# More tiles and filling products around the recurrence of a convolution-attention hybrid

## The chip, the cores and the metric

The kernel runs on one core of one Trainium2 chip. The time is that of one execution on the device in microseconds (us). It was measured three times before the change: 1805.73, 1807.35 and 1809.59 us, median 1807.35. The profile is of one further execution, with a span of 1804.1 us from the first to the last instruction.

## The reference, cut to what matters

```python
# x: 8 x 128 x 48 x 48, N = 48 * 48 = 2304 tokens of 128 channels for each of 8 batches
x = x + causal_attention(group_norm(x))        # layer 0, with projections q, k, v
t = to_tokens(x)                               # 8 x 2304 x 128
t = t + softmax(h @ h.T) @ h                   # layer 1, h = layernorm(t)
# layer 1, the recurrence over the 2304 tokens
Wx  = layernorm(t) @ W.T
Wx  = (Wx - mean) * rsqrt(var + 1e-5) * gamma + beta    # mean, var over all batches and tokens
y_k = sigmoid(Wx_k + y_(k-1) @ V.T),   y_0 = 0
out = t + y
```

Everything is computed in 32-bit floating point.

## The kernel before, in words

**Attention.** Batches follow one another. In each, a causal and then a full attention run over six chunks of 384 queries (`NQ` = 6, `QC` = 384). One list of products (`stream`) is issued with a lag of three items between a score product and its use. The rest of the work (norms, projections, transposes, residuals) hangs in chains of steps, and a planner (`Stream`, `st`) keeps an estimated clock and issues a chain's next step between two products when its due time has come. The numbers in `st.add` and `st.then` are the planner's estimates in us. Nothing reorders the instructions after that: `manual_schedule` keeps the order in which the code issues them, on each engine.

**The last chunks.** `Full.after` builds a chain for each chunk of the full attention: `sums`, `residual` (writes t2, the tokens after layer 1's attention), `rooted` (GpSimd's inverse root for the layer norm), and then, for the last two chunks of the last batch, `keep_last` (transposes t2 to channels by tokens and stores it to `t2_d` in DRAM), `normed`, `back` and `statistics` (the product with W, `wx`, its statistics on VectorE and its copy on ScalarE). The other chunks go by way of DRAM, `spread`, `fetch`, `product`, `stored`. In `product`, chunks 0 and 1 of each batch (the tokens of the recurrence's group 0) are also copied by step into `t2c` by `keep`, and `store` sends them to the output.

**The recurrence.** The 2304 tokens are cut into 96 segments of `LS` = 24 steps, which run side by side in three groups of 32 (`SG`), 8 batches each, so that one step of one group is a product of 128 x 256 columns. Each segment first runs `WARM` = 12 steps over the end of the segment before it, and at the end `seams` compares the states at the cuts; if they disagree, or if a bound on the logits (`bound`, `fl`) is exceeded, a flag makes the kernel take its general path. A step of a group is: TensorE's product into a bank z that VectorE has filled with the normed inputs (`inputs`, two steps at a time), then ScalarE's sigmoid into a tile y.

The results leave in two ways. For group 0 the tokens are already in the output for steps up to `LM` = 20, and GpSimd issues a transfer that adds y, four steps at a time (line 1484). For groups 1 and 2 `add_residual` (line 1458) adds the tokens t2s, loaded back from `t2_d`, on GpSimd into a tile r, two steps at a time, and SyncE sends r (line 1459). Of the last four steps all three groups are added by `add_residual`, on VectorE. SyncE issues its transfers in the order of the code.

The tiles that hold these things are pools with a fixed number of buffers: three tiles y of four steps in group 0, five of two steps in groups 1 and 2, three tiles r for GpSimd and three for VectorE. A writer of a tile waits until the last reader of the buffer is done, a transfer included.

```python
for g in (1, 2, 0):                                       # line 1388
    for b in range(0, B, 4):
        nc.sync.dma_start(t2s[g][:, b : b + 4], t2_d[:, b : b + 4, ts(g, SG * LS)])
```

TensorE's clock is granted by a throttle, at full or half rate. Before the first work of the kernel there are twelve products of the identity with itself (`idle`, line 1329).

Of the kernel before, what the change touches and what calls it, by code (L numbers as in the profile page):

```python
# [14 lines left out]
F32 = mybir.dt.float32  # L15
AF = mybir.ActivationFunctionType
ALU = mybir.AluOpType
AX = mybir.AxisListType
# [10 lines left out]
LOGIT_BOUND = 60.0  # L29
# [575 lines left out]
def fast_path(ctx: ExitStack, tc: tile.TileContext, x, pe, w_ffn, out, x_tok, w_qkv, w_pos, v_t, gamma_beta, flag):  # L605
    nc = tc.nc
    B, C, H, W = x.shape
    N = H * W
    P = 128
# [4 lines left out]
    NQ = N // QC  # L614
    QB = QC // P
    SCALE = 1.0 / math.sqrt(P)
# [5 lines left out]
    dpool = ctx.enter_context(tc.tile_pool(name="dram", bufs=1, space=DRAM))  # L622


    LS = N // SEGS
    SG = SEGS // SEG_GROUPS
    SJ = QC // LS
# [2 lines left out]
    t2_d = dpool.tile([P, B, N], F32, tag="t2_d", name="t2_d")  # L630
    LM = LS - 4

    posb_d = dpool.tile([P, NQ, 3, QC], F32, tag="posb_d", name="posb_d")


# [3 lines left out]
    ident = cpool.tile([P, P], F32, tag="ident", name="ident")  # L639
    make_identity(nc, ident)  # L640
    ones = cpool.tile([P, 1], F32, tag="ones", name="ones")
# [5 lines left out]
    bound = cpool.tile([P, B], F32, tag="bound", name="bound")  # L647
# [12 lines left out]
    with ExitStack() as actx:  # L660
# [9 lines left out]
        work1 = actx.enter_context(tc.tile_pool(name="work1", bufs=1))  # L670
# [6 lines left out]
        def psum_s(name):  # L677
            return ps_s.tile([P, CH], F32, tag="s", name=name)

        def psum_t(name):  # L680
            return ps_t.tile([P, CH], F32, tag="t", name=name)
# [19 lines left out]
        def load_x(b, pieces=2):  # L701
# [12 lines left out]
            out=grp3, in_=grp3, compare_op=ALU.is_ge, fill=0.0, base=0, pattern=[[-cg, GROUPS], [0, cg]], channel_multiplier=1  # L714
        )
        nc.gpsimd.affine_select(
            out=grp3, in_=grp3, compare_op=ALU.is_ge, fill=0.0, base=cg - 1, pattern=[[cg, GROUPS], [0, cg]], channel_multiplier=-1
# [5 lines left out]
            out=triu, in_=triu, compare_op=ALU.is_ge, fill=0.0, base=0, pattern=[[1, P]], channel_multiplier=-1  # L723
# [28 lines left out]
        for r in range(1 - R, R):  # L752
            nc.gpsimd.affine_select(
                out=same, in_=same, compare_op=ALU.not_equal, fill=1.0, base=r * SQ, pattern=[[0, R], [-1, SQ]], channel_multiplier=1
# [4 lines left out]
            out=mine, in_=mine, compare_op=ALU.is_ge, fill=0.0, base=0, pattern=[[0, NQ - 1], [-SQ, R], [0, QB]], channel_multiplier=1  # L759
        )  # L760
        nc.gpsimd.affine_select(
            out=mine, in_=mine, compare_op=ALU.is_ge, fill=0.0, base=SQ - 1, pattern=[[0, NQ - 1], [SQ, R], [0, QB]], channel_multiplier=-1
# [8 lines left out]
        st = Stream()  # L771
# [298 lines left out]
        class Full:  # L1070
# [115 lines left out]
            def after(self, j, o):  # L1186
                b, rows, tsum = self.b, self.rows, self.tsum
# [45 lines left out]
                def rooted():  # L1233
                    c["rs"] = roots[j % 2]
                    nc.gpsimd.tensor_tensor(c["rs"][:, :QB], c["ve"], mhalf, ALU.pow)  # L1235

                def turn_root():
                    nc.vector.transpose(roots_t[j % 2], c["rs"])
# [16 lines left out]
                def product():  # L1255
                    if j < SG // SJ:
                        keep(c["t2x"])
                        st.then(st.now, [("ACT", 0.75)])
                    tp = psum_t(f"wx_{b}_{j}")
                    nc.tensor.matmul(tp[:, :QC], w1T, c["t2x"], start=True, stop=True)  # L1260
                    nc.vector.tensor_mul(c["scale"], tp[:, :QC], c["scale"])
                    nc.vector.bn_stats(stats[:, b * NQ + j, :], c["scale"])

                def stored():
                    store()
                    nc.scalar.copy(wx[:, :, b, ts(j, SJ)], c["scale"].rearrange("p (s l) -> p l s", l=LS))
# [7 lines left out]
                def keep(t2x):  # L1274

                    if before is not None:
                        st.finish(before)
                    if j == 0:
                        self.t2c = work1.tile([P, LM, SG], F32, tag="t2c", name=f"t2c_{b}")
                    nc.scalar.copy(self.t2c[:, :, ts(j, SJ)], t2x.rearrange("p (s l) -> p l s", l=LS)[:, :LM])  # L1280

                def store():
                    if j == SG // SJ - 1:
                        nc.sync.dma_start(out[0, :, :LM, b, :], self.t2c)

                def back():
                    tp = turned_back(c["x2"], f"tx_{b}_{j}")
# [3 lines left out]
                def statistics():  # L1291
                    tp = psum_t(f"wx_{b}_{j}")
                    nc.tensor.matmul(tp[:, :QC], w1T, c["xc"], start=True, stop=True)
                    nc.vector.bn_stats(stats[:, b * NQ + j, :], tp[:, :QC])
                    nc.scalar.copy(wx[:, :, b, ts(j, SJ)], tp[:, :QC].rearrange("p (s l) -> p l s", l=LS))

# [5 lines left out]
                if last:  # L1302
                    steps = [
                        (keep_last, 0.35, [("ACT", 0.5)]),
                        (normed, 0.0, [("DVE", 1.1)]),
                        (back, 0.35, [("ACT", 0.5)]),
                        (statistics, QC * US, [("DVE", 0.55), ("ACT", 0.85)]),
                    ]
                else:
                    steps = [  # L1310
                        (turn_root, 0.0, [("DVE", 0.15)]),
                        (spread, 0.0, [("", 10.0)]),
                        (fetch, 0.0, [("", 9.0)]),
                        (product, QC * US, [("DVE", 1.0)]),
                        (stored, 0.0, [("ACT", 0.85)]),
                    ]
                c["chain"] = self.before["chain"] = st.add([
                    (sums, 0.15, [("DVE", 0.8)]),
                    (residual, 0.35, [("DVE", 3.2)]),
                    (rooted, 0.0, [("POOL", 0.9)]),  # L1320
                    *steps,
                ], max(at, st.free["DVE"]) + 0.2 - st.now)

        norm_chain = {}
        st.add([(ffn_weights, 0.3, [("DVE", 0.5)])], 30.0)

        for i in range(12):
            tp = psum_t(f"idle_{i}")
            nc.tensor.matmul(tp[:, :P], ident, ident, start=True, stop=True)
        for j in range(3):  # L1330
            positions(0, j)
        gn = st.add(group_norm(0))
# [22 lines left out]
        for n in range(len(stream) + LAG):  # L1355
            if n < len(stream):
                part, j, what, first, last = stream[n]
                ready[n] = part.begin(j, what, first)
            if n >= LAG:
                part, j, what, first, last = stream[n - LAG]  # L1360
# [12 lines left out]
    G = SEG_GROUPS  # L1373
    TZ = 2
    TO = [4] + [2] * (G - 1)
    assert LS * SEGS == N and WARM % TZ == 0 and LS % TO[0] == 0 and SG * B * TZ == CH
    with ExitStack() as rctx:
        rc = rctx.enter_context(tc.tile_pool(name="rconst", bufs=1))
        rst = [rctx.enter_context(tc.tile_pool(name=f"rst{g}", bufs=3 if g == 0 else 5)) for g in range(G)]
        rres = rctx.enter_context(tc.tile_pool(name="rres", bufs=3))  # L1380
        ps_z = [rctx.enter_context(tc.tile_pool(name=f"ps_z{g}", bufs=2, space=PSUM)) for g in range(G)]
        ps_w = rctx.enter_context(tc.tile_pool(name="ps_w", bufs=1, space=PSUM))

        rctx.enter_context(tc.manual_schedule())


        t2s = [rc.tile([P, B, SG * LS], F32, tag=f"t2s_{g}", name=f"t2s_{g}") for g in range(G)]
        for g in (1, 2, 0):
            for b in range(0, B, 4):
                nc.sync.dma_start(t2s[g][:, b : b + 4], t2_d[:, b : b + 4, ts(g, SG * LS)])  # L1390
        t2_g = [t.rearrange("p b (s l) -> p l b s", l=LS) for t in t2s]

        zero = rc.tile([P, CH], mybir.dt.bfloat16, tag="zero", name="zero")
        nc.gpsimd.memset(zero, 0.0)

        pw = ps_w.tile([P, CH], F32, tag="w", name="pw")
        nc.tensor.matmul(pw[0:1, :B], ones[:, 0:1], bound, start=True, stop=True)
        fl = rc.tile([1, 4], F32, tag="fl", name="fl")
        nc.vector.reduce_max(fl[:, 0:1], pw[0:1, :B], AX.X)
        nc.vector.tensor_scalar(fl[:, 1:2], fl[:, 0:1], LOGIT_BOUND / SCALE, None, ALU.is_gt)  # L1400


        zs = [deque() for _ in range(G)]
        banks = [deque() for _ in range(G)]
        for t in range(-WARM, -WARM + 2 * TZ, TZ):
            for g in range(G):
                z = ps_z[g].tile([P, TZ, B, SG], F32, tag="z", name=f"z_{g}_{t}")
                nc.tensor.matmul(z.rearrange("p t b s -> p (t b s)"), zero[:, :P], zero, start=True, stop=True)
                banks[g].append(z)

        mv = rc.tile([P, 2], F32, tag="bn_mv", name="bn_mv")
        nc.vector.bn_aggr(mv, stats)
# [40 lines left out]
            nc.vector.tensor_reduce(dm[:, g : g + 1], d[:, g, :, :n], AX.XY, ALU.max, apply_absolute_value=True)  # L1453

        def add_residual(g, l0, yt):
            engine = nc.gpsimd if l0 < LM else nc.vector
            r = rres.tile([P, TZ, B, SG], F32, tag=f"r_{l0 < LM}", name=f"r_{g}_{l0}")
            engine.tensor_add(r, yt, t2_g[g][:, l0 : l0 + TZ])  # L1458
            nc.sync.dma_start(out[g, :, l0 : l0 + TZ], r)

        for t in range(-WARM, LS):
            s = t % TZ
            for g in range(G):
# [12 lines left out]
                if s == TZ - 1:  # L1476
                    zs[g].popleft()

                    l0 = t + 1 - TZ
# [11 lines left out]
        for g in range(G):  # L1491
            add_residual(g, LS - TZ, y[g][:, TO[g] - TZ :])
            if g:
                continue
            nc.tensor.matmul(pw[0:1, P : P + 1], off, ones[:, 0:1], start=True, stop=True)
            nc.vector.tensor_scalar(flag, pw[0:1, P : P + 1], fl[:, 1:2], 0.5, ALU.add, ALU.is_gt)
# [56 lines left out]
```

## Time and profile before

| stretch, us | what runs | TensorE busy | VectorE | ScalarE | GpSimd | granted clock |
|---|---|---|---|---|---|---|
| 0 to 1709.3 | both attentions of 8 batches | 1697.34 | 1233.02 | 702.82 | 178.50 | 1.00 |
| 1709.3 to 1723.3 | last chunk's chain, statistics | 6.94 | 7.05 | 3.19 | 2.69 | 0.61 |
| 1723.3 to 1778.6 | 36 steps of three groups | 51.88 | 45.89 | 41.11 | 28.16 | 0.91 |
| 1778.6 to 1796.1 | last sums, seams, flag | 0.19 | 15.10 | 0.00 | 9.06 | 0.56 |
| 1796.1 to 1804.1 | last transfer, reading the flag, end | 0.00 | 0.01 | 0.00 | 0.00 | 0.50 |

Each row is a stretch of the one profiled execution, with the busy time of the engines in it in us. The granted clock is a mean; 1.00 is the full rate and 0.50 the half one. Busy time beside other busy time costs nothing: what counts in each row is which engine, transfer or wait is the last to let the next row begin. A long busy time is no sign of it by itself.

### The profile page before, as it was taken

The numbers are of one execution on the slowest core, as the hardware profiler recorded it, in microseconds if no ns is written. First come the engines' busy times: TensorE is split into PE (matmuls) and PEld (weight loads), VectorE is DVE, ScalarE is ACT, GpSimd is POOL, SyncE is SP. The second block draws the span as 40 slices with busy tenths as digits, with TensorE's granted clock in tenths as the row PEclk, the third lists the DMA queues.
The fourth block names the chain that finished last, engine by engine and source line by source line (L and its number), as shares of the span: only waits on it lengthen the run. The fifth ranks groups of instructions, "written<-read, shape, count | busy, mean of one in ns | idle before, by whom it ended". The sixth has DMA issues, their size and how long they took to land.

```text
span 1804.1 us, 21863 instructions
## 1 busy us (share of the span) xinstructions
PE 1756.3 (97%) x6291; PEld 1102.3 (61%) x6291; DVE 1301.1 (72%) x3321; ACT 747.1 (41%) x1852; POOL 218.4 (12%) x305
## 2 busy tenths in 40 slices
PE   9999999999999999999999999999999999999893
PEld 5666566666666566665665566665666656665572
DVE  5868678766877678686787668786686767866376
ACT  2344334443344423443245433444335433454362
POOL 1100012000210012000110001100120001200035
PEclk8999999999999999999999999999999999999987
DMA  4205752258304682067513493046720674035776
GB/s 149 103 4 185 202 155 67 92 162 214 112 33 145 177 206 84 17 190 200 139 66 105 153 234 115 6 152 183 193 84 37 190 193 115 27 118 171 174 259 163
DMA packets 173461, 242.43 MB, mean 134 GB/s; under 512 B 62001, under 2 KB 142034, under 8 KB 173332
## 3 DMA queue, kind: packets, MB, share of 16 engines
q1 hardware_dynamic: 172380, 237.93, 44.6%
q0 software_dynamic: 720, 2.62, 1.0%
q8 instruction: 52, 0.85, 0.2%
q14 instruction: 77, 0.63, 0.1%
q10 hardware_dynamic: 232, 0.40, 0.1%
HBM read 144.99 MB, written 95.88 MB: 134 GB/s over the span
## 4 chain that ended last, share of the span: by engine, by line
PE 95%; DVE 2%; DMA 1%; issue 1%; ACT 0%; POOL 0%; SPq 0%; DVEq 0%; ACTq 0%; POOLq 0%
PE s L1166 18%; PE o L1180 18%; PE s L978 17%; PE o L989 16%; PE o L1176 13%; PE pj L869 4%; PE pj L872 2%; PE wx L1260 2%; PE tb L929 1%; PE oc_t L929 1%; PE of_t L929 1%; PE z L1470 1%; DVE r L1458 0%; PE pb L827 0%; DMA out_dram<-r 0%
## 5 line engine op out<-in xcount | busy, mean ns | idle before, releaser
L1168 ACT ACTIVATE p<-s,shift 128x384 f32<-128x384 f32 x504 | 292.2, 580 | 492.6 <-PE s L1166 483.7
L1166 PE MATMUL s<-xh 128*128 128x384 f32 x1008 | 410.3, 489 | 0.0
L980 ACT ACTIVATE p<-s 128x384 f32<-128x384 f32 (+2 forms) x504 | 232.4, 461 | 425.8 <-PE s L978 391.7
L1180 PE MATMUL o<-p,xhT 128*128 128x384 f32 x1008 | 403.9, 487 | 4.4 <-ACT p L1168 4.4
L978 PE MATMUL s<-q,k 128*128 128x384 f32 (+2 forms) x1008 | 381.1, 460 | 0.1
L989 PE MATMUL o<-p,vT 128*128 128x384 f32 (+2 forms) x1008 | 377.6, 456 | 0.0
L1176 PE MATMUL o<-g,xhT 128*128 128x384 f32 x720 | 281.2, 488 | 0.8 <-DMA g<-e 0.8
L1180 PEld LDWEIGHTS o<-p,xhT 128*128 128x128 f32 x1008 | 189.0, 190 | 132.2 <-ACT p L1168 8.7
L989 PEld LDWEIGHTS o<-p,vT 128*128 128x128 f32 x1008 | 188.8, 190 | 114.7 <-issue 0.6
L1166 PEld LDWEIGHTS s<-xh 128*128 128x128 f32 x1008 | 186.1, 190 | 115.0
L1004 DVE TENSOR_TENSOR acc<-acc,p 128x384 f32<-128x384 f32 (+2 forms) x408 | 211.0, 517 | 48.8 <-ACT p L980 17.9
L978 PEld LDWEIGHTS s<-q,k 128*128 128x128 f32 x1008 | 180.6, 191 | 90.5 <-issue 0.5
L1129 DVE STREAM_TRANSPOSE t<-p 128x384 f32<-128x384 f32 x360 | 187.2, 550 | 37.5 <-ACT p L1168 34.6
L1176 PEld LDWEIGHTS o<-g,xhT 128*128 128x128 f32 x720 | 133.2, 190 | 82.9 <-issue 1.7
L1137 DVE TENSOR_REDUCE tsum<-t 128x12 f32<-128x1152 f32 x120 | 162.4, 1353 | 4.2
L874 DVE TENSOR_TENSOR z<-pj,pb 128x384 f32<-128x384 f32 x144 | 79.0, 549 | 103.5 <-PE pj L869 87.7
L983 POOL TENSOR_TENSOR p<-p,triu 128x128 f32<-128x128 f32 x144 | 83.5, 587 | 545.8 <-ACT p L980 434.4
L1235 POOL TENSOR_TENSOR roots<-ve_f,mhalf 128x3 f32<-128x3 f32 x48 | 40.7, 849 | 552.5 <-DVE ve_f L913 552.5
L1168 ACT ACTIVATION_READ_ACCUMULATOR p<-s,shift 128x1 f32 x504 | 97.2, 193 | 0.0
L869 PE MATMUL pj<-xn,wT 128*128 128x384 f32 x192 | 79.8, 500 | 1.4 <-DVE xn L862 1.4
L919 POOL TENSOR_TENSOR rs_c<-ve_c,mhalf 128x3 f32<-128x3 f32 x48 | 46.9, 976 | 245.7 <-DVE ve_c L913 245.7
L1222 DVE SCALAR_TENSOR_TENSOR t<-of_t,ri,t1t 128x128 f32<-128x128 f32 x144 | 41.5, 344 | 33.2 <-PE of_t L929 33.2
(257 smaller groups left out, 1485.7 us busy)
## 6 DMA issues: line engine op xcount, KB each, us to landing
e<-t SPq DMA_DIRECT2D x120, 576.0 KB
g<-e SPq DMA_DIRECT2D x480, 144.0 KB
pb<-posb_d SPq DMA_DIRECT2D x46, 576.0 KB
t1t<-in_x_tok_dram SPq DMA_DIRECT2D x48, 192.0 KB
t2s<-t_d SPq DMA_DIRECT2D x6, 1536.0 KB
t_d<-tt SPq DMA_DIRECT2D x184, 48.0 KB
t2x<-t_d SPq DMA_DIRECT2D x46, 192.0 KB
scale<-rs SPq DMA_DIRECT2D x46, 192.0 KB
```

What stands on the lines that cost most here:

```text
L869: nc.tensor.matmul(ps[:, :QC], wT[:, j, :], xn, start=True, stop=True)
L978: nc.tensor.matmul(s[:, off:QC], keys[b][:, ts(m, P)], queries[b, j][:, off:], start=True, stop=True)
L980: nc.scalar.activation(p[:, off:], s[:, off:QC], AF.Exp, scale=SCALE)
L983: nc.gpsimd.tensor_mul(p[:, off : off + P], p[:, off : off + P], triu)
L989: nc.tensor.matmul(o[:, off:QC], vals[b][:, ts(m, P)], p[:, off:], start=first, stop=last)
L1004: nc.vector.tensor_add(a[:, off:], a[:, off:], p[:, off:])
L1129: nc.vector.transpose(t[:, :, :, g, :].rearrange("p b j r -> p j b r"), p.rearrange("p (j b r) -> p j b r", j=QB, b=R))
L1137: nc.vector.tensor_reduce(self.tsum[j][:, n - j - 1, :], t.rearrange("p b j m r -> p (b j) (m r)"), AX.X, ALU.add)
L1166: nc.tensor.matmul(s[:, :QC], xh[:, ts(m, P)], xh[:, ts(j, QC)], start=True, stop=True)
L1168: nc.scalar.activation(p, s[:, :QC], AF.Exp, bias=shift, accum_out=self.rows[:, m, j : j + 1])
L1176: nc.tensor.matmul(out_ap, xhT[:, QB * i + g, :], p, start=first, stop=last)
L1180: nc.tensor.matmul(o[:, :QC], xhT[:, what[1], :], p, start=first, stop=last)
```

## The change

It is meant to take waits out of the recurrence and of the stretch before it, and to keep TensorE's clock at its full rate there. It has these parts:

- In the two gaps of the last chunk's chain, and between the clearing of the banks z and the first step, products of the identity are issued on TensorE: 14, 8 and 14 of them. The twelve at the start stay, in one tile of another pool.
- The product for the logits' bound and the two VectorE instructions that read it move from before the statistics' sum to behind the first inputs.
- `t2c` keeps all 24 steps; the copy has 384 elements a partition instead of 320, and the planner's cost for it goes from 0.75 to 0.85. The last four steps are stored by step in `t2l_d`. The recurrence loads them as `t2l`, so t2s is not loaded for group 0, and group 0's adds on VectorE read contiguous tokens.
- Group 0 has four tiles y instead of three, groups 1 and 2 have six instead of five, GpSimd's results have six tiles r instead of three; VectorE's three are in a pool of their own.

```diff
+    t2l_d = dpool.tile([P, LS - LM, B, SG], F32, tag="t2l_d", name="t2l_d")
...
                 def rooted():
                     c["rs"] = roots[j % 2]
                     nc.gpsimd.tensor_tensor(c["rs"][:, :QB], c["ve"], mhalf, ALU.pow)
+                    if b == B - 1 and j == NQ - 1:
+                        idle(psum_s("idle_last"), 14)
...
-                        st.then(st.now, [("ACT", 0.75)])
+                        st.then(st.now, [("ACT", 0.85)])
...
-                        self.t2c = work1.tile([P, LM, SG], F32, tag="t2c", name=f"t2c_{b}")
-                    nc.scalar.copy(self.t2c[:, :, ts(j, SJ)], t2x.rearrange("p (s l) -> p l s", l=LS)[:, :LM])
+                        self.t2c = work1.tile([P, LS, SG], F32, tag="t2c", name=f"t2c_{b}")
+                    nc.scalar.copy(self.t2c[:, :, ts(j, SJ)], t2x.rearrange("p (s l) -> p l s", l=LS))
...
-                        nc.sync.dma_start(out[0, :, :LM, b, :], self.t2c)
+                        nc.sync.dma_start(out[0, :, :LM, b, :], self.t2c[:, :LM])
+                        nc.sync.dma_start(t2l_d[:, :, b, :], self.t2c[:, LM:])
...
                     nc.tensor.matmul(tp[:, :QC], w1T, c["xc"], start=True, stop=True)
+                    if b == B - 1 and j == NQ - 1:
+                        idle(psum_s("idle_last2"), 8)
                     nc.vector.bn_stats(stats[:, b * NQ + j, :], tp[:, :QC])
...
-        for i in range(12):
-            tp = psum_t(f"idle_{i}")
-            nc.tensor.matmul(tp[:, :P], ident, ident, start=True, stop=True)
+        def idle(tp, n):
+
+            for _ in range(n):
+                nc.tensor.matmul(tp[:, :P], ident, ident, start=True, stop=True)
+
+        idle(psum_s("idle"), 12)
...
-        rst = [rctx.enter_context(tc.tile_pool(name=f"rst{g}", bufs=3 if g == 0 else 5)) for g in range(G)]
-        rres = rctx.enter_context(tc.tile_pool(name="rres", bufs=3))
+        rst = [rctx.enter_context(tc.tile_pool(name=f"rst{g}", bufs=4 if g == 0 else 6)) for g in range(G)]
+        rres = rctx.enter_context(tc.tile_pool(name="rres", bufs=6))
+        rlast = rctx.enter_context(tc.tile_pool(name="rlast", bufs=3))
...
-        for g in (1, 2, 0):
+        for g in range(1, G):
             for b in range(0, B, 4):
                 nc.sync.dma_start(t2s[g][:, b : b + 4], t2_d[:, b : b + 4, ts(g, SG * LS)])
+        t2l = rc.tile([P, LS - LM, B, SG], F32, tag="t2l", name="t2l")
+        nc.sync.dma_start(t2l, t2l_d)
...
-        nc.tensor.matmul(pw[0:1, :B], ones[:, 0:1], bound, start=True, stop=True)
-        fl = rc.tile([1, 4], F32, tag="fl", name="fl")
-        nc.vector.reduce_max(fl[:, 0:1], pw[0:1, :B], AX.X)
-        nc.vector.tensor_scalar(fl[:, 1:2], fl[:, 0:1], LOGIT_BOUND / SCALE, None, ALU.is_gt)
...
                 banks[g].append(z)
+        idle(pw[:, 2 * P :], 14)
...
         def add_residual(g, l0, yt):
-            engine = nc.gpsimd if l0 < LM else nc.vector
-            r = rres.tile([P, TZ, B, SG], F32, tag=f"r_{l0 < LM}", name=f"r_{g}_{l0}")
-            engine.tensor_add(r, yt, t2_g[g][:, l0 : l0 + TZ])
+            engine, pool = (nc.gpsimd, rres) if l0 < LM else (nc.vector, rlast)
+            r = pool.tile([P, TZ, B, SG], F32, tag="r", name=f"r_{g}_{l0}")
+            t2 = t2s[g].rearrange("p b (s l) -> p l b s", l=LS)[:, l0 : l0 + TZ] if g else t2l[:, l0 - LM : l0 - LM + TZ]
+            engine.tensor_add(r, yt, t2)
             nc.sync.dma_start(out[g, :, l0 : l0 + TZ], r)
+
+
+        nc.tensor.matmul(pw[0:1, :B], ones[:, 0:1], bound, start=True, stop=True)
+        fl = rc.tile([1, 4], F32, tag="fl", name="fl")
+        nc.vector.reduce_max(fl[:, 0:1], pw[0:1, :B], AX.X)
+        nc.vector.tensor_scalar(fl[:, 1:2], fl[:, 0:1], LOGIT_BOUND / SCALE, None, ALU.is_gt)
```

More of the change, by code (lines that the diff above doesn't have):

```diff
@@ L1384, in fast_path @@
         rctx.enter_context(tc.manual_schedule())
-        t2s = [rc.tile([P, B, SG * LS], F32, tag=f"t2s_{g}", name=f"t2s_{g}") for g in range(G)]
-        for g in (1, 2, 0):
+        t2s = [None] + [rc.tile([P, B, SG * LS], F32, tag=f"t2s_{g}", name=f"t2s_{g}") for g in range(1, G)]
+        for g in range(1, G):
             for b in range(0, B, 4):
                 nc.sync.dma_start(t2s[g][:, b : b + 4], t2_d[:, b : b + 4, ts(g, SG * LS)])
-        t2_g = [t.rearrange("p b (s l) -> p l b s", l=LS) for t in t2s]
+        t2l = rc.tile([P, LS - LM, B, SG], F32, tag="t2l", name="t2l")
+        nc.sync.dma_start(t2l, t2l_d)
         zero = rc.tile([P, CH], mybir.dt.bfloat16, tag="zero", name="zero")
```

## The prediction

> **What bounds the kernel now.** I read the page's busy line first: TensorE is busy 97% of the span, so the two attention layers, up to 1709.3 us, are TensorE's and little is to be had there. Then I read the end of the chain of waits, because the change works there. Its columns are start, duration, engine, output and line.
>
> ```profile
> 1710.49 0.87 DVE t L1222 x3
> 1712.92 0.85 POOL roots L1235
> 1714.20 1.00 PE tx L937 x3
> 1715.81 1.66 PE wx L1293 x2
> 1719.19 1.37 DVE bn_mv L1412
> 1722.07 0.81 DVE z_-12_14095 L1432
> 1723.36 1.19 PE z_-12_14095 L1470 x2
> ...
> 1788.12 3.72 DMA out_dram<-r
> 1791.86 1.44 DVE r L1458
> 1794.69 1.42 DVE r L1458
> ```
>
> From 1709.3 to 1723.4 TensorE waits in a serial chain; then 108 recurrence steps run; the very end is a transfer of r, three VectorE adds and an 8.0 us close to 1804.1. Next I asked for busy time by stretches, to see the granted clock (the last three columns are clock, DMA share and GB/s; PE busy comes first).
>
> ```profile
> 1708.93:1712.34 3.41, 1.80 (x8) 0.73 (x6) 1.78 (x8) 0.96 (x2) 0.00 (x0) 1.00 0.00 0
> 1712.34:1715.75 3.41, 0.99 (x3) 0.54 (x3) 1.22 (x6) 0.47 (x1) 1.37 (x2) 0.50 0.16 58
> ...
> 1725.99:1729.41 3.42, 3.42 (x9) 2.70 (x8) 2.93 (x6) 1.53 (x4) 0.00 (x0) 0.50 1.03 404
> 1729.41:1732.82 3.41, 3.41 (x17) 2.99 (x16) 2.15 (x5) 2.84 (x8) 0.00 (x0) 1.00 1.03 402
> ```
>
> The clock is halved from 1712.34 to 1729.41: the last gaps of layer 1 lose it, and the first seven step products take 0.85 us apart instead of 0.43. Then the timeline of GpSimd, ScalarE and VectorE in the recurrence (a bracket is the idle time before, and what ended it):
>
> ```profile
> 1744.86 3.02 POOL L1458 TENSOR_TENSOR r<-y,t2s 128x512 f32<-128x512 f32 x2 [22.71 <-ACT y L1472]
> 1755.03 1.52 POOL L1458 TENSOR_TENSOR r<-y,t2s 128x512 f32<-128x512 f32 x1 [1.65 <-DMA out_dram<-r]
> 1763.83 1.52 POOL L1458 TENSOR_TENSOR r<-y,t2s 128x512 f32<-128x512 f32 x1 [1.96 <-ACT y L1472]
> 1771.91 0.94 ACT L1472 ACTIVATE y<-z 128x256 f32<-128x256 f32 x3 [3.39 <-DMA out_dram<-y]
> 1772.63 1.52 POOL L1458 TENSOR_TENSOR r<-y,t2s 128x512 f32<-128x512 f32 x1 [1.98 <-ACT y L1472]
> 1784.39 3.27 POOL L1458 TENSOR_TENSOR r<-y,t2s 128x512 f32<-128x512 f32 x2
> 1791.86 1.44 DVE L1458 TENSOR_TENSOR r<-y,t2s 128x512 f32<-128x512 f32 x1 [2.22 <-DMA out_dram<-r]
> ```
>
> GpSimd is the recurrence's real limit. It has 20 adds and 5 transfer issues, and four adds plus one issue last 4 x 1.58 + 0.6 = 6.95 us, while TensorE needs 12 x 0.431 = 5.2 us for the same four steps. GpSimd also loses 1.65 + 1.96 + 1.98 = 5.6 us in three waits. The last two are put down to ScalarE, whose y was done long before; each stands at the fourth add of a row, like the first, so I read all three as waits for a result tile (three of them) still being sent out. ScalarE's 3.39 us wait at 1768.5 is group 0's state tile (three of them). SyncE's queue is in order: the last steps' results, ready earlier, leave only after GpSimd's last add at 1787.66.
>
> **What the Trainium skill says.** "TensorE: Matmul & The Clock Gate", part 1: the clock is set by free-running windows of 3.413 us. The trace agrees: 1712.34 to 1729.41 is 17.07 us, five windows. A window busy 1.77 us of 3.41 (1702.10 on) kept the clock, 1.80 with gaps inside (modelled ends included) lost it, and one busy 2.63 did not restore it. [...] t2s steps by 24, and 512 elements took 1.42 us when VectorE was undisturbed[...]. "VectorE: DVE Perf Modes", "Two Vector instructions with no wait between them", names the second SBUF read interface as shared with GpSimd: three adds took 7.30 us beside GpSimd's adds, 2.43 each against 1.42.
>
> **The change, part by part.**
>
> (1) Products of the identity. One is two instructions; the 24 at the kernel's start took 4.98 us and the next product ran at the full rate, so they count as activity. At the full rate I take 128/384 of a 384-column pair's 0.64 us, 0.213 us. The first 14 (2.99 us) come behind the transposes that end at 1710.45: to 1713.4. Queued behind them are the three tk transposes (0.33 us), ended by 1713.8; these delay only ScalarE's copy and the store of the last tokens by about 2 us, which nobody needs until 1740. The path's tx waits for VectorE until 1714.2 anyway, so nothing is lost. The clock stays, and wx takes 0.81 instead of 1.65, tx about 0.1 less: statistics end about 1717.03 instead of 1718.06.
>
> (2) The moved bound check. Its product and two VectorE instructions stood ahead of the statistics' sum: 1718.06 to 1719.12, 1.06 us. Moved behind the first inputs they cost VectorE 0.35 us there, hidden as reckoned in (3).
>
> (3) The first step. From 1717.06 the old durations give sum 1.43, root and coefficients 1.41, inputs 1.2: group 0 could start at about 1721.3. But TensorE has 8 products (from 1716.3, to 1718.0), 6 clearing products of 512 columns (0.213 each, to 1719.3) and 14 more (to 1722.3); the step is queued behind them and starts at 1722.35. VectorE bounds it alike: inputs of steps -12 and -10 with the check between end at 1725.5, which lets the stream start no sooner than about 1722.2. At the full clock from there, it compares with the old stream run back from 1729.44 by seven pairs: 1729.44 - 7 x 0.431 = 1726.42. Gain 1726.42 - 1722.35 = 4.1 us; GpSimd's first add moves from 1744.86 to about 1740.8.
>
> (4) More tiles. Six result tiles give a transfer five adds (7.9 us) to land instead of two; the three waits go, 5.6 us. Four state tiles in group 0 mean that the tile for step 20 was sent with steps 4 to 7, issued about 10 us after the first add and landed 6.4 us later, and wanted 22.9 us after it: no wait. That takes the 3.39 us from ScalarE and the half clock after it (1773.8 to 1777.2), both off the end's path while GpSimd is later. Six tiles in groups 1 and 2: step 22's needs GpSimd's twelfth add, done at +20.8, wanted at +25.9.
>
> GpSimd's work is then 20 x 1.58 + 5 x 0.6 = 34.6 us, plus about 2.7 beside VectorE's last adds and comparisons. (Before: 1787.66 - 1744.86 = 42.8, less 5.6 in waits, is 37.2, the same sum.) It ends at 1740.8 + 37.3 = 1778.1, where TensorE is done at 1769.5.
>
> (5) Group 0's last tokens by step. No load of 2 x 1.5 MB; it ran until 1740 beside steps that didn't need it, so worth nothing. VectorE's two group 0 adds take about 0.68 us instead of 1.42 (0.55 was paid for 384 contiguous elements); only the one at the end counts: 0.75 us. In the layers, 16 ScalarE copies have 384 elements instead of 320, 0.97 to 1.15 us, 2.9 us in all on an engine busy 41%, beside TensorE; the planner's 0.75 to 0.85 can shift a step of a chain by one place. Eight stores of 128-byte rows cost SyncE 0.4 us each behind an equal one (0.40). I take zero; the bounds are 2 us either way, TensorE's idle time left in the layers being some 3 us.
>
> (6) The end: last GpSimd add to VectorE's 4.2 us as before, adds 3.5 instead of 4.25, close 8.0. Sum: 4.1 + 5.5 + 0.75 = 10.35 us; 1807.35 - 10.35 = 1797.0.
>
> **Rivals.** *A, results limited by transfers (0.17):* from 1746 to 1764.8 the DMA engines were 74% busy; the same bytes in 6.95 instead of 8.75 us make 93%, so landings may stretch and half of the 5.5 us come back: 1799.8. For it: that share. Against: six tiles absorb it, and it is under 100%. *B, more (0.08):* VectorE's shorter, earlier adds collide less with GpSimd, and the 2.7 us go: 1794.3. *C, the clock falls all the same (0.07):* then 28 filling and clearing products from 1717.3 last 3.4 + 2.6 + 6.0, the start slips to 1729.3, 2.9 later than 1726.42: 1807.35 + 2.9 - 6.25 = 1804.0. Against: from 1710.45 on TensorE has no hole over 0.6 us. *D, slower (0.06):* the larger copies, small-row stores and shifted plan starve TensorE in the layers; each batch would have to lose over 1.3 us to eat 10.35, and with 1.7 it ends at 1810. Against: TensorE waits almost nowhere there and ScalarE idles 59%.
>
> **How the numbers follow.** The forecast has 0.62. Its neighbours A and B reach 1794.3 to 1799.8; with a run's spread (1805.73 to 1809.59 before) and the layers' 2 us either way I take 1792.5 to 1802.5, which leaves out C and D and a little more. Faster by over 0.2% (3.6 us) holds for the forecast, A, B and most of C: 0.92; same 0.03; slower 0.05.
>
> **What would show it.** Right: clock 1.00 from 1709 to the end of the steps; first step about 1722.3; first GpSimd add about 18.4 us later; no wait for r before GpSimd's adds, none for y before ScalarE; GpSimd's last add about 37 us after its first; group 0's add near 0.7 us; VectorE's last add still waiting for a transfer of r behind GpSimd. Wrong: GpSimd still waiting for r, half-clock steps, or attention ending later than 1710.

## The result, and the profile after

In the first comparison the changed kernel took 1795.25 us (1794.24 to 1796.92, 4 runs) and the kernel before 1807.21 us (1805.73 to 1809.59, 4 runs): ratio 0.9933, interval 0.9916 to 0.9951. In a later group of runs on one chip it was 1796.08 against 1806.1 us, ratio 0.9944, interval 0.9928 to 0.9960. So it is 10 to 12 us faster, some 0.6%.

First the chain of waits of the changed kernel, its last rows; the columns are as before (start, duration, engine, output, line).

```profile
1712.64 0.87 DVE t L1224 x3
1715.07 0.85 POOL roots L1237
1716.35 0.86 PE tx L939 x3
1717.82 0.91 PE wx L1298 x2
1718.73 1.80 PE idle_last L1336 x16
1722.02 3.12 PE pw L1336 x28
1741.01 28.58 PE z L1483 x132
1770.01 2.72 POOL r L1465
1772.74 2.78 DMA out_dram<-r
1775.53 5.42 DVE r L1465 x2
1785.81 1.42 DVE r L1465
```

Two things are new. The filling products (`idle_last`, `pw` L1336) are themselves on the path to the first step. And VectorE's last adds no longer wait for a transfer. The chain still names one, of r at 1772.74, ahead of VectorE's adds at 1775.53, but VectorE was at work on an earlier add until then, as its timeline below shows. Now the granted clock, from busy time by stretches (first number TensorE's busy time; the last three are clock, DMA share and GB/s):

```profile
1709.30:1723.30 14.00, 12.46 (x81) 9.51 (x80) 7.04 (x24) 3.68 (x6) 2.69 (x6) 1.00 0.37 129
1723.30:1773.20 49.90, 48.87 (x235) 42.37 (x233) 45.00 (x63) 41.41 (x108) 29.45 (x23) 1.00 0.77 225
```

The clock is full from the end of attention to the last step, where the two rows of the table before had 0.61 and 0.91. Then GpSimd's timeline in the recurrence:

```profile
1743.75 3.00 POOL L1465 TENSOR_TENSOR r<-y,t2s 128x512 f32<-128x512 f32 x2 [21.34 <-ACT y L1485]
1746.68 1.08 POOL L1497 DMA_DIRECT2D out_dram<-y  x1
1747.48 6.26 POOL L1465 TENSOR_TENSOR r<-y,t2s 128x512 f32<-128x512 f32 x4
1753.39 1.20 POOL L1497 DMA_DIRECT2D out_dram<-y  x1
...
1772.94 2.08 POOL L1497 DMA_DIRECT2D out_dram<-y  x1
1773.55 6.09 POOL L1465 TENSOR_TENSOR r<-y,t2s 128x512 f32<-128x512 f32 x2
```

No add waits for a tile any more: four adds follow each other without a gap, and the issues come 6.5 us apart instead of 8.7. (The records of GpSimd adds in a row overlap: the starts lie 1.48 us apart, so I compare from start to start.) And VectorE at the end:

```profile
1769.17 6.44 DVE L1465 TENSOR_TENSOR r<-y,t2l 128x512 f32<-128x512 f32 x1 [0.35 <-ACT y L1485]
1775.53 5.42 DVE L1465 TENSOR_TENSOR r<-y,t2s 128x512 f32<-128x512 f32 x2
1780.86 0.41 DVE L1456 TENSOR_TENSOR d<-y,warm 128x248 f32<-128x248 f32 x1
...
1783.74 0.68 DVE L1465 TENSOR_TENSOR r<-y,t2l 128x512 f32<-128x512 f32 x1
```

The same add of contiguous tokens takes 0.68 us when GpSimd is done and 6.44 us while GpSimd adds without a gap. The Trainium skill, "SBUF — State Buffer", "Who interferes with whom", says that a VectorE instruction with two SBUF inputs and a GpSimd instruction that reads SBUF exclude each other. The trace agrees, and shows more: if the add's own 0.68 us are the last of its 6.44, it did not get in behind the GpSimd add that was running but only behind three more of them.

Where the time went, by stretches that do not depend on when attention ended (us, one profiled execution each):

| | before | after | |
|---|---|---|---|
| end of attention's last product to GpSimd's first add | 35.52 | 32.26 | -3.26 |
| GpSimd's first add to the end of its last | 42.80 | 35.89 | -6.91 |
| from there to the end of VectorE's last add | 8.44 | 7.59 | -0.85 |
| from there to the end of the span | 8.00 | 6.57 | -1.43 |
| sum | 94.76 | 82.31 | -12.45 |

In these two executions attention itself ended at 1709.34 and 1711.49 us. The changed kernel, profiled again, had 1709.63: this is no effect of the change (below).

### The profile page after: what moved, and what is told of

It is laid out like the page before. It is cut to its first block, busy times and chain, and to the rows that moved or that the text cites. A ratio compares the mean times of both kernels' runs of the same rounds, so it can differ in the third digit from the quotient of the medians.

```text
span 1793.8 us, 22009 instructions
## 1 busy us (share of the span) xinstructions
PE 1757.0 (98%) x6363; PEld 1106.4 (62%) x6363; DVE 1298.0 (72%) x3321; ACT 751.6 (42%) x1852; POOL 217.0 (12%) x305
## 4 chain that ended last, share of the span: by engine, by line
PE 95%; DVE 2%; DMA 1%; SPq 1%; issue 1%; ACT 0%; POOL 0%; DVEq 0%; ACTq 0%; POOLq 0%
PE s L1168 18%; PE o L1182 18%; PE s L980 17%; PE o L991 16%; PE o L1178 12%; PE pj L871 4%; PE pj L874 2%; PE z L1483 2%; PE wx L1264 2%; PE oc_t L931 1%; PE tb L931 1%; PE of_t L931 1%; SPq L1102 1%; DVE r L1465 0%; PE pb L829 0%
```

## The experiments

In what follows a **tail** is the sum of the table above, from the end of attention's last product to the end of the span; it is free of what happens at the start. The changed kernel's two profiles have tails of 82.31 and 82.57 us; their first three parts agree within 0.03 us, and the difference is in the last one. The ratios are of times to those of the kernel before on the same chip in the same group of runs, each with its interval.

### The changed kernel once more

> The changed kernel itself, on the chip of the runs of this group. All theories: a ratio of 0.9933 to 0.994 to the kernel before. It also shows how far the end of the attentions moves between two executions of one program: 1709.3 to 1711.6 was seen in six traces, and if it is the program (larger copies, small-row stores) it comes at 1711.5 again; if it is the start of the execution, it may come anywhere in that range.

1796.08 us against 1806.1, ratio 0.9944 (0.9928 to 0.9960), tail 82.57. Attention ended at 1709.63. Its first store of t2c, early in the kernel, came at 209.91 us, against 211.91 in the first profile, so all of the 1.86 us between the two executions of one program was there after the first batch. Over all fourteen traces that store came anywhere from 208.5 to 213.2 us, and the way from it to the end of attention took 1498.6, 1499.1 and 1499.5 us in the three with the old tokens and 1498.4 to 1501.2 in the others. The start of an execution moves by more than anything that the change does to the layers.

The traces also show what goes with it, the clock. These are the first 60 us of the executions with the earliest and the latest store (`e9_both`, 208.5, and `e3_old_tiles`, 213.2):

```profile
0.00:60.00 60.00, 53.59 (x212) 35.12 (x213) 36.20 (x81) 18.46 (x40) 11.02 (x37) 0.94 0.43 150
0.00:60.00 60.00, 54.52 (x194) 35.12 (x195) 33.37 (x73) 16.97 (x36) 10.52 (x37) 0.86 0.42 143
```

After its first full-rate stretch TensorE spent 6.83 us of them at half rate in the one and 17.07 in the other. In the fourteen traces the store comes at 208.5 us with 6.83 us at half rate, at 209.4 to 210.5 with 10.24, at 210.8 to 211.9 with 13.65 and at 212.8 to 213.2 with 17.07. By an estimate from the first and the last of these figures, 10.24 us more at half rate cost TensorE 5.1 us if it is busy throughout, against 4.7 seen. Why the clock falls oftener in one execution than in another stays open.

### Without the filling products

```diff
-                    if b == B - 1 and j == NQ - 1:
-                        idle(psum_s("idle_last"), 14)
...
-                    if b == B - 1 and j == NQ - 1:
-                        idle(psum_s("idle_last2"), 8)
...
-        idle(pw[:, 2 * P :], 14)
```

> The changed kernel without its three sets of filling products (14, 8 and 14); the twelve at the start stay. My theory: the clock falls to half in the last gaps of layer 1, the statistics come about 1 us later, the first step starts near 1724.6 in place of 1725.2 (nothing stands in front of it), but the first seven pairs run at 0.85 us apart, so GpSimd's first add comes about 2.5 us later than 1743.75 and the time is about 1797.8 (ratio to before 0.9947). Rival: the 14 products in front of the first step cost as much as the clock brings, and the time stays at 1795.3 (0.9933).

1795.53 us, ratio 0.9944 (0.9932 to 0.9957), tail 84.09. The time cannot tell it from the changed kernel; the trace can. In TensorE's timeline (the first steps), and in the busy time by stretches with the clock:

```profile
1724.97 0.67 PE L1478 MATMUL z_-12_14093<-y,vT_f 128*128 128x256 f32 x2
...
1726.67 1.06 PE L1478 MATMUL z_-12_14091<-y_-12_14134,vT_f 128*128 128x256 f32 x2
...
1729.08 0.60 PE L1478 MATMUL z_-10_14097<-y_-12_14134,vT_f 128*128 128x256 f32 x2
```

```profile
1715.27:1722.10 6.83, 5.19 (x13) 1.99 (x13) 3.03 (x6) 2.24 (x3) 1.30 (x3) 0.50 0.67 232
1722.10:1725.51 3.41, 1.21 (x4) 0.59 (x4) 2.98 (x8) 0.38 (x1) 1.01 (x4) 1.00 1.03 410
1725.51:1728.92 3.41, 3.36 (x9) 2.64 (x9) 3.34 (x8) 1.45 (x4) 0.00 (x0) 0.50 1.03 394
```

Without the products the clock falls, but only some four step products run at half rate here and not seven as before: the clock came back for one stretch of 3.41 us in between, which it did not do in the profile before. One execution does not show how often it does. From the end of attention to GpSimd's first add it takes 33.62 us instead of 32.26. So the filling products were worth 1.4 us beside the moved check in this execution, not the 2.5 that I expected.

### Only the filling products

```diff
+                    if b == B - 1 and j == NQ - 1:
+                        idle(psum_s("idle_last"), 14)
...
+                    if b == B - 1 and j == NQ - 1:
+                        idle(psum_s("idle_last2"), 8)
...
+        idle(pw[:, 2 * P :], 14)
```

> The kernel before with only the three sets of filling products. My theory: the steps run at the full clock from the first, GpSimd's first add comes 2 to 3 us earlier, GpSimd's waits for its result tiles stay, so the time is about 1804.7 (ratio 0.9986). Rival: the whole gain comes from the clock, then 1796 to 1798 (0.994 to 0.995).

1804.09 us, ratio 0.9993 (0.9984 to 1.0001), tail 92.71. The clock is at 1.00 from the end of attention until 1769.14, where it falls in a wait of ScalarE for a transfer, which stays; the first add comes 32.76 us after attention instead of 35.52, 2.8 us earlier, and GpSimd's three waits (1.88, 1.82 and 1.90 us) stay. Of the tail 2.05 us are saved, of 12.45 in the changed kernel. The clock is not where most of the gain comes from.

### The check at its old place

```diff
+        nc.tensor.matmul(pw[0:1, :B], ones[:, 0:1], bound, start=True, stop=True)
+        fl = rc.tile([1, 4], F32, tag="fl", name="fl")
+        nc.vector.reduce_max(fl[:, 0:1], pw[0:1, :B], AX.X)
+        nc.vector.tensor_scalar(fl[:, 1:2], fl[:, 0:1], LOGIT_BOUND / SCALE, None, ALU.is_gt)
...
+        idle(pw[:, 2 * P :], 14)
...
-        nc.tensor.matmul(pw[0:1, :B], ones[:, 0:1], bound, start=True, stop=True)
-        fl = rc.tile([1, 4], F32, tag="fl", name="fl")
-        nc.vector.reduce_max(fl[:, 0:1], pw[0:1, :B], AX.X)
-        nc.vector.tensor_scalar(fl[:, 1:2], fl[:, 0:1], LOGIT_BOUND / SCALE, None, ALU.is_gt)
```

(The line of the filling products is in both kernels; it stands in the diff to show the order.)

> The changed kernel with the product for the logits' bound and its two VectorE instructions at their old place, ahead of the statistics' sum. My theory: the sum comes about 1.4 us later, but the first step was held by the 14 filling products, and only VectorE's inputs for the second pair of steps get 0.35 us late, so GpSimd's first add comes some 0.3 to 0.4 us later (32.6 us after the end of attention in place of 32.25), and the time cannot be told from the changed kernel's. Rival, the prediction's step 2 taken alone: the whole 1.06 us or more comes back.

1795.6 us, ratio 0.9943 (0.9930 to 0.9957), first add 32.75 us after attention, tail 82.88: 0.5 us later where 0.3 to 0.4 was expected. The first step did start with its inputs this time (ready 1725.34, step 1725.49). With the runs before, the two edits make a square, from the end of attention to GpSimd's first add:

| us | check at the old place | check moved |
|---|---|---|
| no filling products | 35.52 | 33.62 |
| filling products | 32.76 | 32.26 |

They do not add: the difference between the columns is 1.9 us without the filling products and 0.5 with them. The first step itself shows why. Without the products it comes 14.02 us after attention with the check at the old place and 12.95 with the check moved, 1.07 us earlier; with them it comes after 13.68 and 13.71, so these hold it in its place. The other 0.8 of the 1.9 us come after the first step, where fewer step products fell into half-rate stretches; with one execution in each field it stays open whether that is the check's doing or chance. The tiles do not matter here: with the check at the old place, the filling products gave 32.76 us with the old tiles and 32.75 with the new ones.

### Fewer filling products

```diff
-        idle(pw[:, 2 * P :], 14)
+        idle(pw[:, 2 * P :], 6)
```

> The changed kernel with 6 in place of 14 filling products in front of the first step. My theory: the inputs of the first step are ready 1.7 us before TensorE gets to it, behind the filling products, and VectorE's check waits behind them too; with eight fewer (1.8 us) the first step comes about 1.5 us earlier after the end of attention, the clock stays full, and GpSimd's first add and the time come about 1 us earlier. Rival: the clock is lost without the other eight, and the time grows by 1 to 2 us.

1794.07 us, ratio 0.9931 (0.9915 to 0.9947; the intervals overlap), tail 81.22. In the changed kernel the first step's inputs were ready at 1723.48 and TensorE came to it at 1725.20; here they are ready at 1722.97 and the step starts at 1723.11. After attention the step comes 1.58 us earlier than with 14, and the first add, at 31.33 us, 0.93 us earlier, as expected; the clock stays. In this trace fourteen were too many by about a microsecond.

### The old numbers of tiles

```diff
-        rst = [rctx.enter_context(tc.tile_pool(name=f"rst{g}", bufs=4 if g == 0 else 6)) for g in range(G)]
-        rres = rctx.enter_context(tc.tile_pool(name="rres", bufs=6))
+        rst = [rctx.enter_context(tc.tile_pool(name=f"rst{g}", bufs=3 if g == 0 else 5)) for g in range(G)]
+        rres = rctx.enter_context(tc.tile_pool(name="rres", bufs=3))
```

> The changed kernel with the old numbers of tiles: three results for GpSimd, three state tiles in group 0, five in groups 1 and 2. My theory: GpSimd waits three times about 1.9 us for its result tiles again, its last add ends some 42 us after its first instead of 35.9, and the time is about 1801 (ratio 0.9965). Rival: the results are limited by the transfers or by VectorE at the end whatever the tiles, then no more than 1 us of it comes back: 1796 (0.9938).

1802.39 us, ratio 0.9981 (0.9972 to 0.9991), tail 89.06. GpSimd's timeline, the adds that waited:

```profile
1754.02 1.52 POOL L1465 TENSOR_TENSOR r<-y,t2s 128x512 f32<-128x512 f32 x1 [1.62 <-DMA out_dram<-r]
...
1762.97 1.52 POOL L1465 TENSOR_TENSOR r<-y,t2s 128x512 f32<-128x512 f32 x1 [2.12 <-DMA out_dram<-r]
...
1771.44 1.52 POOL L1465 TENSOR_TENSOR r<-y,t2s 128x512 f32<-128x512 f32 x1 [1.65 <-ACT y L1485]
...
1780.48 1.81 POOL L1465 TENSOR_TENSOR r<-y,t2s 128x512 f32<-128x512 f32 x1 [2.23 <-DMA out_dram<-r]
```

The waits are back, 7.6 us of them, and the stretch from first to last add is 42.23 us. One is again put down to ScalarE's y, at the place where its neighbours name the transfer of r: the reading of the profile before was right.

### The old numbers of state tiles alone

```diff
-        rst = [rctx.enter_context(tc.tile_pool(name=f"rst{g}", bufs=4 if g == 0 else 6)) for g in range(G)]
+        rst = [rctx.enter_context(tc.tile_pool(name=f"rst{g}", bufs=3 if g == 0 else 5)) for g in range(G)]
```

> The changed kernel with six result tiles but the old numbers of state tiles (three, five, five). My theory: the state tiles are off the path of the end; ScalarE may wait up to 1 us for group 0's tile at step 20, GpSimd does not notice, and the time stays within 1 us of 1795.3 (ratio 0.993 to 0.994). Rival: ScalarE's 3.39 us wait was worth its length, then 1798 to 1799 (0.995).

1794.2 us, ratio 0.9940 (0.9926 to 0.9953), tail 82.63, first to last add 35.90. The state tiles make no difference; ScalarE does not wait for a transfer either, since with six result tiles GpSimd issues group 0's transfers early enough. The 3.39 us wait of ScalarE before was a symptom of GpSimd's delay. The whole gain of the tiles is that of GpSimd's six result tiles.

### Group 0's last tokens as before

```diff
-        t2s = [None] + [rc.tile([P, B, SG * LS], F32, tag=f"t2s_{g}", name=f"t2s_{g}") for g in range(1, G)]
-        for g in range(1, G):
+        t2s = [rc.tile([P, B, SG * LS], F32, tag=f"t2s_{g}", name=f"t2s_{g}") for g in range(G)]
+        for g in (1, 2, 0):
...
-        t2l = rc.tile([P, LS - LM, B, SG], F32, tag="t2l", name="t2l")
-        nc.sync.dma_start(t2l, t2l_d)
```

The larger copy and the store of `t2l_d` are undone with it, and the state tiles are three, five and five.

> The changed kernel with group 0's last tokens as before (t2s loaded for group 0, t2c of 20 steps, no small-row stores) and, for room, the old numbers of state tiles, which made no difference by themselves. My theory: only VectorE's last add of group 0 is on the path, 1.42 in place of 0.68 us, so 0.7 to 0.8 us slower than the changed kernel. Rival: the close after VectorE's last add, 8.0 and 8.2 us in the two traces with the old tokens and 6.4 to 7.0 in the others, hangs on it as well, and it is 2 us slower; second rival: without the stores, which hold SyncE 2.3 to 3.6 us each, the attentions end earlier and nothing is lost.

1795.87 us, ratio 0.9947 (0.9935 to 0.9959), tail 84.94. The times do not tell it from the changed kernel (0.9944 and 0.9933). The one trace is 2.4 us longer in the tail: 0.8 in GpSimd's stretch, 0.74 from there to VectorE's end, 0.8 to 1.1 in the close. The close took 8.00, 8.22 and 7.70 us in the three traces with the old tokens and 6.42 to 6.96 in the seven others where VectorE's add comes last and the output is whole. I have no cause for the close, and the times do not confirm it. The 0.74 us are the add of strided tokens, 1.43 us in place of 0.68, as expected. This part also makes room: group 0's t2s takes 24 KB a partition and t2l 4 KB, and the six result tiles need 12 KB. But this run has both the old tokens and six result tiles, so the gain of the tiles did not need that room.

### Half of GpSimd's adds

```diff
-                        if t < LS - 1:
+                        if t < LS - 1 and g == 2 and l0 < LM:
+                            nc.sync.dma_start(out[g, :, l0 : l0 + TZ], y[g][:, so + 1 - TZ : so + 1])
+                        elif t < LS - 1:
                             add_residual(g, l0, y[g][:, so + 1 - TZ : so + 1])
```

> The changed kernel in which group 2's results up to step 20 are sent without their tokens: y goes straight out, so ten of GpSimd's 20 adds are left out, with the same bytes sent. My theory: GpSimd is what bounds the recurrence; with ten adds and five issues (18 us) it keeps up with TensorE, VectorE's adds are not held up any more, its last add ends about 35 us after GpSimd's first in place of 43.5, and the time falls by about 8 us, ratio about 0.990. Rival: the transfers bound it (the DMA engines were 89% busy from 1745 to 1773), then it falls by less than 3 us.

1788.24 us, ratio 0.9909 (0.9895 to 0.9923), tail 75.62. VectorE's timeline at the end:

```profile
1767.27 0.69 DVE L1465 TENSOR_TENSOR r<-y,t2l 128x512 f32<-128x512 f32 x1 [0.35 <-ACT y L1485]
1767.88 2.77 DVE L1465 TENSOR_TENSOR r<-y,t2s 128x512 f32<-128x512 f32 x2
...
1775.09 0.69 DVE L1465 TENSOR_TENSOR r<-y,t2l 128x512 f32<-128x512 f32 x1 [1.57 <-DMA out_dram<-r]
```

This kernel leaves out group 2's tokens up to step 20. GpSimd keeps up with TensorE, and VectorE's three adds take 3.4 us where they took 11.8. The tail is 7 us shorter, the time 6 us by the two ratios (0.9944 and 0.9909). This shows both claims at once: GpSimd bounds the way from the steps to the end, and its adds hold up VectorE's. The steps themselves it does not bound: TensorE's last one ends 60.7 us after attention in the changed kernel and here. It also shows what comes next: the DMA engines are busy all the time from 1744 to 1772 (mean busy share 1.03, against 0.89 in the changed kernel over nearly the same stretch), and VectorE's last adds wait 1.57 us for a transfer.

### Some last adds as products

```diff
+            nc.tensor.matmul(z, ident, yt, start=True, stop=False)
+            nc.tensor.matmul(z, ident, t2, start=False, stop=True)
+            nc.scalar.copy(r, z)
+            nc.scalar.dma_start(out[g, :, l0 : l0 + TZ], r)
...
+        add_by_product(2, LM, held)
+        for g in range(G):
+            add_by_product(g, LS - TZ, y[g][:, TO[g] - TZ :])
```

> The changed kernel with four of the six last adds (group 2's steps 20 and 21, every group's steps 22 and 23) as two products of the identity each on TensorE, y and then the tokens into one bank, a ScalarE copy and a transfer issued by ScalarE; the six tiles of the last results in one pool. My theory: GpSimd and VectorE hold each other up at the end, and VectorE's chain of adds and comparisons and the in-order transfers behind GpSimd's last add set it; TensorE and ScalarE are idle from 1772.6. Four adds take TensorE about 7 us, to 1779.5; VectorE has two adds less beside GpSimd and none after the comparisons, so the flag comes about 3 us earlier and the time falls by 3 to 5 us, to about 0.9915. Rival: the end is set by GpSimd's last add alone (1779.6) and what follows it in SyncE's queue, then no more than 1 us; or strided tokens are slow to stream into TensorE and the time grows.

1791.18 us, ratio 0.9922 (0.9905 to 0.9939), tail 80.72. It gains 4 us by the ratios, whose intervals overlap, but in the tail only 1.9 us where 3 to 5 were expected. TensorE's timeline shows why:

```profile
1773.27 1.02 PE L1466 MATMUL zr<-t2l,ident 128*128 128x512 f32 x2
1774.13 1.02 PE L1465 MATMUL zr<-y,ident 128*128 128x512 f32 x2
1774.99 2.72 PE L1466 MATMUL zr<-t2s,ident 128*128 128x512 f32 x2
...
1781.06 0.19 PE L1522 MATMUL pw<-ones,off 128*1 128x1 f32 x2
```

A product streams y and the tokens t2l, which are contiguous, in 1.02 us and the tokens t2s, which step by 24 words, in 2.72, at the full clock. The product for the flag stands behind them in TensorE's queue, 1.5 us after its operand is ready at 1779.51.

### Both: fewer filling products, last adds as products

```diff
-        idle(pw[:, 2 * P :], 14)
+        idle(pw[:, 2 * P :], 6)
...
+        add_by_product(2, LM, held)
+        for g in range(G):
+            add_by_product(g, LS - TZ, y[g][:, TO[g] - TZ :])
```

> The changed kernel with both: 6 filling products in front of the first step, and four of the last adds on TensorE and ScalarE. My theory: the two gains add, 4 to 6 us less than the changed kernel, ratio about 0.991. Rival: the earlier start only makes GpSimd's queue longer, then no less than the run with the products at the end alone.

1791.45 us, ratio 0.9916 (0.9900 to 0.9933), tail 79.76: 0.96 less than with the products at the end alone. The times of these two runs are the same. Against the changed kernel on the same chip (interval 0.9928 to 0.9960) it is likely the better kernel, by 2.8 us of tail and 4.6 us in the medians, at the low end of the 4 to 6 expected.

### Group 2's last add back on VectorE

The edit is shown against the kernel of the run above.

```diff
-        for g in range(G):
+        for g in range(2):
             add_by_product(g, LS - TZ, y[g][:, TO[g] - TZ :])
...
+            add_residual(2, LS - TZ, y[2][:, TO[2] - TZ :])
             nc.vector.tensor_scalar(flag, pw[0:1, P : P + 1], fl[:, 1:2], 0.5, ALU.add, ALU.is_gt)
```

> The run with 6 filling products and products at the end, but with group 2's last add back on VectorE behind the comparisons. My theory: streaming tokens with a step of 24 words took TensorE 2.57 us for two instructions in place of 0.86, so the product for the flag stood 1.5 us behind the last add in TensorE's queue; now the flag comes about 0.3 to 0.5 us earlier, and the time is the same as or up to 1 us less than with four adds as products (1791.3). Rival: VectorE's extra add delays the flag and the last transfer, then up to 1 us more.

1791.63 us, ratio 0.9927 (0.9914 to 0.9940), tail 78.00, 1.8 less than with four adds as products, where up to 1 was expected. The time is the same as that run's; which of the two is better stays open.

## Why the prediction was right or wrong, point by point

- **What bounds the end: GpSimd, through its result tiles.** Shown. With the old tiles again the first-to-last stretch is 42.23 us, with the old state tiles alone 35.90, with half of the adds the tail falls by 7 us. In the changed kernel GpSimd limits the results and not the steps, so "the recurrence's real limit" says too much. The predicted gain of 5.5 us was 6.9, because two sizes were off. I took 4.76 / 3 = 1.58 us for one add; four adds and an issue last 6.52 us and not 6.95, so one add is about 1.48. And I took the waits at the idle time printed before the adds, 5.6 us. From start to start, GpSimd's rows before are longer by more than that:

```profile
1748.63 4.76 POOL L1458 TENSOR_TENSOR r<-y,t2s 128x512 f32<-128x512 f32 x3
...
1757.11 4.76 POOL L1458 TENSOR_TENSOR r<-y,t2s 128x512 f32<-128x512 f32 x3
...
1765.90 4.75 POOL L1458 TENSOR_TENSOR r<-y,t2s 128x512 f32<-128x512 f32 x3
...
1774.70 9.14 POOL L1458 TENSOR_TENSOR r<-y,t2s 128x512 f32<-128x512 f32 x4
```

The three rounds with a wait, from the start of one of these rows to that of the next, took 8.48, 8.79 and 8.80 us, 6.5 more than three of 6.52. The rest of the 6.9 is collision with VectorE (see the rivals).
- **State tiles off the path.** Shown: worth nothing alone.
- **The clock and the first step.** The clock stayed as forecast. The gain to GpSimd's first add was 3.26 us instead of 4.1. The step that was short is the queue in front of the first step: 13.71 us from the end of attention instead of 13.0. The 14 products took 3.12 us and not 2.99, and the clearing products started 0.4 us later than reckoned. The prediction saw that the filling products hold the first step; eight fewer give back 0.93 us. (Its sum for group 0's inputs comes to 1721.1 and not 1721.3; nothing hangs on it.)
- **The moved check.** 1.06 us was its gain in the prediction's account of VectorE. Without the filling products the first step does come 1.07 us earlier; with them in place the step stays, and 0.5 us is left at GpSimd's first add.
- **Group 0's last tokens and the layers.** Taken at zero in the layers: no difference larger than the spread from one execution to the next. But "SyncE 0.4 us each" was wrong: a store of `t2l_d` holds SyncE's queue for 2.3 to 3.8 us in the eleven traces that have it, as its timeline shows in the first batch of the changed kernel. And TensorE's idle time, put at some 3 us in the layers, is 5.2 us in the profile before from 100 to 1700 us alone.

```profile
211.91 0.41 SPq L1288 DMA_DIRECT2D out_dram<-t2c  x1
212.37 2.73 SPq L1289 DMA_DIRECT2D t2l_d<-t2c  x1
215.20 2.22 SPq L1102 DMA_DIRECT2D g<-e  x4
```

- **The end.** Predicted 0.75 us for the contiguous add: 0.85 measured from GpSimd's last add to VectorE's end, of which the run with the old tokens gives 0.74 back. The 4.2 us in front of these adds stayed at 4.1 by luck: before, 2.22 of them were a wait for a transfer of r; now no last add waits for one, and VectorE's held-up adds and its comparisons fill the time. VectorE's first add of group 0 did not take 0.68 us but 6.44. The close was held constant at 8.0 and was 6.6 and 6.9 in the changed kernel's two profiles, unexplained. The sum is -3.26 - 6.91 - 0.85 - 1.43 = -12.45 against -10.35. That it came as near as this is in part luck too: the forecast had 0.8 us too much at the first step, against 1.4 too little in GpSimd's stretch and the 1.4 of the close.
- **The rivals.** Transfers as the limit: not here, they are the next limit once GpSimd has half of its adds. More through less collision at the end: hardly. Before, the fourth round, from 1774.70 to 1784.39, took 9.69 us, 3.2 more than one without VectorE; after, the last two adds took 6.09 us where they had taken 3.27, 2.8 more. So 0.4 us went, and not 2.7. The clock lost all the same, and a slower attention: neither.

## What to carry to other kernels

When an engine off the main path writes to tiles that are sent out, count how many of its instructions fit into one landing; too few tiles make it wait at every turn, and the profile may put that wait down to the wrong engine. A wait of another engine (here ScalarE's 3.39 us) can be a mere symptom of it: undo one pool at a time. Products that only keep TensorE's clock must end before the operands of the real ones are ready, and edits in one gap need not add.

## What the runs showed of the hardware that was not expected

- An add on VectorE with two SBUF operands took 6.41 to 6.48 us beside back-to-back GpSimd adds, in nine traces, and 0.69 us beside none. If its own 0.69 us come last, the GpSimd add that was running and three more went first.
- Streamed through TensorE, 512 columns that step by 24 words took 2.72 us for the two instructions of a product, contiguous ones 1.02 us (full clock).
- A store of 128-byte rows held the issuing queue 2.3 to 3.8 us when it came right behind another one of such rows, which itself took 0.40 us in most cases.
- The start of an execution moved a fixed point early in the kernel by up to 4.7 us (208.5 to 213.2) between executions, which is some two fifths of what the change is worth. It went with the time that TensorE spent at half rate in the first 60 us, 6.83 to 17.07 us.
